# A gated recurrence followed by a binary feed-forward layer: one visit for four input chunks, another order in three iterations, paired blocks at the end, one more idle product

## The chip, the core and the metric

The kernel runs on one core of a Trainium2 chip. A core has TensorE (PE: matrix products into PSUM; its weight loads are shown as PEld), VectorE (DVE), ScalarE (ACT), GpSimd (POOL) and SyncE (SP). Each works through its own queue in order, and they wait for each other by semaphores. Transfers between the main memory and the on-chip memory SBUF are issued by SyncE and ScalarE and carried by 16 DMA engines. The metric is the device time of one execution in microseconds (us), lower being better; the figure to be predicted is the median over the runs.

## What is computed

The input x has 2 sequences of 4096 tokens of 256 numbers. The first layer is a gated recurrence with 64 states, the second a feed-forward layer with binary weights; each has a residual and a layer norm.

```python
u = x @ W_in + b_in                       # 256 -> 64
g = sigmoid(x @ W_gate + b_gate)          # 256 -> 256
h_t = tanh(h_{t-1} @ A + u_t @ Bm)        # along each sequence
y_t = g_t * (h_t @ C.T + u_t @ D.T) + (1 - g_t) * x_t
x1 = layernorm(2 * x + y @ W_out + b_out)
h = gelu(x1 @ (alpha1 * sign(w1)).T + b1) # 256 -> 1024
out = layernorm(x1 + h @ (alpha2 * sign(w2)).T + b2)
```

## The kernel before

**Tiling.** Each sequence is cut into 64 segments of 64 tokens, and all segments of both sequences advance together. One step of the recurrence is then one product for 128 columns (`steps`, line 156) and one tanh on ScalarE (line 158), and step after step depends on the one before. 48 warm-up steps over the last three quarters of each segment give the start states (`first_states`, line 161, copies them), and 64 steps follow: 112 in all. If a comparison at the end (`compare`, lines 166 to 172) finds that the warm-up was too short, a slow branch redoes everything; it is not taken here. The work beside the recurrence is cut into 16 chunks of 512 columns, each four positions of all segments.

**A chunk's work** is a list of pieces: u (line 131, read out of PSUM by VectorE in line 144), gates (line 313, tanh in line 361), `mix` (the y product, line 370, and the subtraction d, line 377), `mix_end`, `project` (W_out in two halves, line 395; then x1 and its statistics, line 406 and class `Stats`), `shift` and `norm` (layer norm; ScalarE, line 279), `turn` (transposes, line 423; ScalarE copies the high part xhi, line 431, VectorE subtracts to get the low part xlo, line 433), `rest` (adds b2 on GpSimd), four times `up` (products with sign(w1), line 451; gelu, line 458; high part hhi, line 467), `low` (low part hlo on VectorE, line 474) and `down` (products with sign(w2), line 490; after the last, VectorE scales out of PSUM into o, line 506), and at last `add` (line 512), `stats` and `store` (line 281 or 279, output in line 527). High and low parts keep single precision with a faster product format. The input of mix goes through a tile hu, which two transfers fill from the states (upper half) and from u (lower half), lines 342 to 349.

**PSUM.** The pool p_1 has three buffers, which u, gates and up share. p_m has one: mix, project and turn take turns in it, and each waits until the one before has been read. p_2 has one, for down.

**Order.** TensorE, ScalarE, VectorE and GpSimd run in the order in which the code emits (line 629); SyncE's queue is ordered by the compiler. `emit` (line 601) puts steps between pieces: each piece adds its cost (a table: a u visit 2000, a part of the gates 640, others 860) to a counter, and when it passes a pace one step is emitted, if u of its chunk is there. In the early stage the pace is 500, so that each part of a gate and each visit of u is followed by one step; later it is 5600. When 4, 8 and 12 of the 64 steps are out, the hu transfers of chunks 0, 1 and 2 are issued.

**Stages.** At the start six idle products (line 154) run while the first input and W_in load. Then seven rounds follow (lines 636 to 655): one part of the gates, a visit of u for a pair of chunks, x loads, and parts of the gates; on VectorE the weights are made into signs (`prepare_w`). The order of the pairs is (5, 6), (7, 8), (9, 10), (11, 12), (13, 14), (15, 0), (1, 2). After the first mixes and projections the main loop runs with c from 0 to 14: up, low, down of chunks c and c-1, mix of c+2, turn of c+1, project of c+2. In iterations 1 to 12 the gates of a later chunk stand behind the addition and statistics of chunk c-1. The last chunk, 15, ends in `down_end`, which works on one block of 128 rows at a time: products, scale, addition (GpSimd for the first three blocks, VectorE for the last), statistics of the block before, store of the one before that.

Of the kernel before, what the change touches and what calls it, by code (L numbers as in the profile page):

```python
# [19 lines left out]
KH = H // P  # L20
# [7 lines left out]
TB = N // P  # L28
# [4 lines left out]
EARLY = 500  # L33
# [4 lines left out]
def gated_recurrence_then_binary_ffn(  # L38
# [16 lines left out]
    nc = tc.nc  # L55
# [68 lines left out]
    def u_of_chunks(*chunks):  # L124

        n = N * len(chunks) // 2
        parts = [(chunks[0], 0), (chunks[1], 0) if len(chunks) == 2 else (chunks[0], 1)]
        ps = p_1.tile([P, N], FP, tag="h", name=f"ps_u{chunks[0]}")
        for k in range(KD):
            for (c, i), r in zip(parts, (LOW, TOP)):  # L130
                nc.tensor.matmul(  # L131
                    ps[r, :n],
                    w_in[k],
                    x_tiles[c][:, k, bass.ts(i, n)],
                    start=k == 0,
                    stop=k == KD - 1,
                    skip_group_check=True,
                )
        for (c, i), r in zip(parts, (LOW, TOP)):
            to = u_of[:, bass.ds(c * SPC + i * n // W, n // W)].rearrange("p j b k -> p (j b k)")  # L140
            if r is TOP and c == FIRST:
                nc.scalar.activation(to, ps[r, :n], AF.Identity, bias=bin_c[r, :])
            else:
                nc.vector.tensor_scalar(to, ps[r, :n], bin_c[r, :], None, ALU.add)
        have_u.update(chunks)
        yield
# [4 lines left out]
    def idle_products(n):  # L151

        for _ in range(n):
            nc.tensor.matmul(p_h, ones, ones, start=True, stop=True)
# [174 lines left out]
    class Chunk:  # L329
# [180 lines left out]
        def add(self, blocks=range(TB), engine=nc.vector):  # L510
            cut = slice(blocks[0], blocks[-1] + 1)
            engine.tensor_tensor(
                self.x1[:, cut, :], self.x1[:, cut, :], self.o[:, cut, :], ALU.add
            )
            yield
# [27 lines left out]

        def down_end(self):

            self.st2 = Stats(self.x1, f"b{self.nm}")
            for tb in range(TB + 2):
                one, before = range(tb, tb + 1), range(tb - 1, tb)
                if tb < TB:
                    for j in range(KH // 2, KH):  # L550
                        self.down_part(j, tb)
                    self.scale(one)
                    yield from self.add(one, nc.gpsimd if tb < TB - 1 else nc.vector)
                if 1 <= tb <= TB:
                    for what in (self.st2.gather, self.st2.merge, self.st2.root):
                        what(before)
                if tb >= 2:
                    engine = nc.scalar if tb < TB else nc.vector
                    queue = nc.scalar if tb % 2 else nc.sync
                    yield from self.store(range(tb - 2, tb - 1), engine, queue)  # L560

        def redo(self):

# [37 lines left out]
    def emit(what, pieces, pace=5600):  # L601
        nonlocal since
        for _ in pieces:
            since += COST.get(what, 0)
            if since >= pace:
                since = min(since - pace, pace // 2)
                if ready():
                    next_steps()

    def do(i, what, *args, pace=5600):  # L610
        if not 0 <= i < len(ch):
            return
        if what == "load":
            need = WARM + (ch[i].c + 1) * SPC
            while done < need:
                next_steps()
            ch[i].load()
        elif what in ("load_x", "load_gate_x"):
            getattr(ch[i], what)()
        else:  # L620
            emit(what, getattr(ch[i], what)(*args), pace)
# [7 lines left out]
    with tc.manual_schedule(engines={ET.PE, ET.Activation, ET.DVE, ET.Pool}):  # L629
        waiting = []  # L630
        for c in range(FIRST + 1, FIRST + 6):
            load_xT(c)
        idle_products(6)
        emit("u", u_of_chunks(FIRST), 1 << 30)
        since = 0
        pairs = [(5, 6), (7, 8), (9, 10), (11, 12), (13, 14), (15, 0), (1, 2)]
        loads = [[10, 11], [12, 13], [14, 15, 0], [1, 2], [3], [], []]
        for n, pair in enumerate(pairs):
            before = 2 if n == 0 else 1
            parts(before, EARLY)  # L640
            emit("u", u_of_chunks(*pair), EARLY)
            for c in loads[n]:
                load_xT(c)
            if n == 0:
                load_weights()
            if n == 3:
                halve_weights()
            if n >= 5:
                load_xT(n + 3)
            for i in range(7 - before):  # L650
                if 1 <= n < 5 and i == 0:
                    load_w(n - 1)
                if 2 <= n < 6 and i == 3:
                    prepare_w(n - 2)
                parts(1 if (n, i) != (6, 5) else 0, EARLY)
        assert done >= WARM + SPC, done
        emit("u", u_of_chunks(3), EARLY)
        for i in range(4):
            ch[i].xt = x_tiles[i]
        do(0, "mix", pace=850)  # L660
        do(0, "mix_end")
        parts(1, 600)
        assert done >= WARM + 2 * SPC, done
        do(1, "mix", pace=850)
        do(1, "mix_end")
        parts(1, 600)
        do(0, "project", 0, p_2, "o", pace=1700)
        do(0, "project", 1, pace=1700)
        assert done >= WARM + 3 * SPC, done
        do(2, "mix", pace=1700)  # L670
        do(0, "shift")
        do(1, "project", 0, p_2, "o", pace=1700)
        do(0, "norm")
        do(1, "project", 1, pace=1700)
        mixed = ch[2].mix_end()
        next(mixed)
        parts(2, 1700)
        while waiting:
            next_steps()
        waiting = None  # L680
        do(0, "turn", True)
        emit("", mean_w2())
        do(1, "norm", nc.vector)
        do(0, "rest")
        next(mixed)
        parts(2, 1700)
        for i in (4, 5):
            do(i, "load_x")
        end = len(ch) - 1
        parts_met = compare()  # L690
        late = gates(ch[10:], TB)
        for c in range(end):
            do(c + 6, "load_x")
            if c % 2 == 0:
                do(10 + c // 2, "load_gate_x")
            do(c, "up", 0)
            do(c, "low", 0)
            do(c - 1, "down", 2)
            do(c + 3, "load")
            if c > 0:  # L700
                do(c + 1, "shift")
                do(c + 1, "norm")
                do(c + 2, "mix")
                do(c + 2, "mix_end")
            do(c, "up", 1)
            do(c - 1, "down", 3)
            do(c - 1, "add", range(TB), nc.gpsimd if c == end - 1 else nc.vector)
            if c < end - 1:
                do(c - 1, "stats")
            if 1 <= c <= 12:  # L710
                emit("gate", (next(late, None) for _ in range(KD)))
            do(c + 1, "turn")
            do(c, "low", 1)
            do(c + 1, "rest")
            do(c, "up", 2)
            do(c, "low", 2)
            if c == end - 1:
                do(c - 1, "stats")
            else:
                do(c - 1, "store")  # L720
            if c == end - 2:
                assert done == len(plan), done
                next(parts_met)
                next(parts_met)
            do(c, "down", 0)
            do(c + 2, "project", 0)
            do(c, "up", 3)
            do(c, "down", 1)
            do(c, "low", 3)
            if c == end - 1:  # L730
                do(c - 1, "store")
            do(c + 2, "project", 1)
            if c == end - 2:
                next(parts_met)
                next(parts_met)
        count()
        do(end, "up", 0)
        do(end, "low", 0)
        do(end - 1, "down", 2)
        do(end - 1, "down", 3)  # L740
        do(end, "up", 1)
        do(end - 1, "add")
        do(end - 1, "stats")
        do(end, "low", 1)
        do(end, "up", 2)
        do(end, "low", 2)
        do(end, "down", 0, True)
        do(end, "up", 3, True)
        do(end - 1, "store", range(TB), nc.scalar)
        do(end, "low", 3, True)  # L750
        do(end, "down", 1)
        do(end, "down_end")
# [64 lines left out]
```

## Time and profile before

| | before |
|---|---|
| median of 3 runs | 452.75 us (452.65 to 454.31) |
| the profiled execution | 453.36 us, span 451.5 us |
| mean granted TensorE clock | 0.995 |
| TensorE busy | 439.7 us, 97% of the span |
| VectorE busy | 358.0 us, 79% |
| ScalarE busy | 261.1 us, 58% |
| GpSimd busy | 176.2 us, 39% |
| memory traffic | 44.51 MB, mean 99 GB/s |

The profile is of one execution. Its span runs from the first to the last event that it holds; the device time is 1.86 us longer. In a timeline line the first number is the start in us from the span's start, the second the duration in us (for several instructions joined in one line, until the end of the last); then come the engine (with q for a queue that issues transfers), the line of the kernel, the operation, the tile written and those read, shapes, and how many instructions the line joins. In brackets stands the idle time before it and what ended that. A product in plain single precision leaves two records for each call.

### The profile page before, as it was taken

What the parts mean: (1) busy time and instruction counts of PE and PEld (TensorE: products, weight loads), DVE (VectorE), ACT (ScalarE), POOL (GpSimd) and SP (SyncE); (2) the same over time, 40 slices, a digit from 0 to 9 for tenths busy, and PEclk for the clock granted to TensorE, in tenths of its full rate; (3) what the DMA queues carried; (4) which work ended last, traced back from release to release, by engine and by line L of the source; (5) the groups of instructions that cost most, each with busy time, mean ns of one, the idle gap of its engine ahead of it and who ended that gap; (6) DMA issues with size and microseconds to landing.
All of it is one profiled execution on the core that took longest, in us unless ns stands there. A gap on an engine that the chain in (4) does not pass through costs nothing.

```text
span 451.5 us, 6729 instructions
## 1 busy us (share of the span) xinstructions
PE 439.7 (97%) x2504; PEld 357.6 (79%) x2504; DVE 358.0 (79%) x600; ACT 261.1 (58%) x424; POOL 176.2 (39%) x179
## 2 busy tenths in 40 slices
PE   8999999999999999999999999999999999989992
PEld 5665666788888888887978787979788888879982
DVE  0245737976989798989898988899898989896775
ACT  2343442485657575757574747566666656556772
POOL 1001300553545434343445454535353545451713
PEclk9999999999999999999999999999999999999997
DMA  8898814321133322322232312212112020201012
GB/s 302 267 330 305 292 36 137 102 83 23 48 105 106 107 59 94 116 94 70 93 103 70 105 52 89 76 52 67 47 37 81 13 93 1 93 1 48 1 46 100
DMA packets 14838, 44.51 MB, mean 99 GB/s; under 512 B 2000, under 2 KB 3024, under 8 KB 14800
## 3 DMA queue, kind: packets, MB, share of 16 engines
q1 hardware_dynamic: 14224, 43.65, 29.1%
q8 instruction: 22, 0.36, 0.3%
q10 hardware_dynamic: 576, 0.37, 0.3%
q14 instruction: 16, 0.13, 0.1%
HBM read 31.43 MB, written 8.39 MB: 88 GB/s over the span
## 4 chain that ended last, share of the span: by engine, by line
PE 92%; DVE 5%; DMA 1%; ACT 1%; issue 0%; POOLq 0%; POOL 0%
PE ps_h L451 25%; PE ps_o L490 24%; PE ps_z L395 12%; PE ps_g L313 12%; PE ps_y L370 6%; PE ps_s L157 6%; PE ps_u L131 4%; PE ps_t L423 3%; DMA wab<-in_W_in_AB 1%; DVE bs_b L256 1%; DVE hlo L474 1%; DVE d L382 1%; DVE d L377 1%; DVE xlo L433 1%; DVE o L506 0%; PE ps_p L490 0%
## 5 line engine op out<-in xcount | busy, mean ns | idle before, releaser
L458 ACT ACTIVATE h<-ps_h,bias_c,al 128x512 f32<-128x512 f32 x128 | 97.5, 775 | 80.4 <-PE ps_h L451 75.2
L490 PE MATMUL ps_o<-sg,hhi 128*128 128x256 f32 x496 | 120.3, 282 | 0.0
L490 PE MATMUL ps_o<-sg,hlo 128*128 128x256 f32 x496 | 119.0, 279 | 0.1
L474 DVE TENSOR_TENSOR hlo<-h,hhi 128x1024 fp32r<-128x1024 f32 (+1 forms) x65 | 84.5, 1318 | 23.6 <-ACT hhi L467 23.5
L490 PEld LDWEIGHTS ps_o<-sg,hhi 128*128 128x128 f32 x496 | 93.6, 189 | 2.3
L490 PEld LDWEIGHTS ps_o<-sg,hlo 128*128 128x128 f32 x496 | 93.4, 188 | 2.5 <-DVE hlo L474 0.3
L451 PE MATMUL ps_h<-xhi,sg 128*128 128x512 f32 x256 | 92.2, 441 | 0.0
L451 PE MATMUL ps_h<-xlo,sg 128*128 128x512 f32 x256 | 80.2, 394 | 0.2
L355 POOL TENSOR_TENSOR xn<-xn,bo_r 128x256 f32<-128x256 f32 x64 | 59.3, 957 | 48.4 <-DMA xn<-in_x 48.4
L355 POOL TENSOR_TENSOR xn<-xn,b_r 128x256 f32<-128x256 f32 x64 | 75.5, 1208 | 1.2 <-PE ps_t L423 1.2
L467 ACT CAST hhi<-h 128x1024 fp32r<-128x1024 f32 (+1 forms) x65 | 67.3, 1037 | 2.0
L313 PE MATMUL ps_g<-xt,w_gate 128*128 128x384 f32 (+3 forms) x208 | 67.9, 438 | 0.0
L266 POOL TENSOR_TENSOR rs_a<-rs_a,neg_half 128x4 f32<-128x4 f32 x16 | 17.2, 1076 | 122.2 <-DVE rs_a L265 103.4
L395 PE MATMUL ps_z<-w_out,tg 128*128 128x256 f32 x256 | 61.1, 380 | 1.5 <-DVE xlo L433 1.5
L158 ACT ACTIVATE st<-ps_s 64x128 f32<-64x128 f32 x112 | 30.0, 267 | 56.0 <-PE ps_s L157 55.6
L451 PEld LDWEIGHTS ps_h<-xlo,sg 128*128 128x128 f32 x256 | 48.1, 188 | 11.9 <-DVE xlo L433 0.9
L157 PEld LDWEIGHTS ps_s<-st,wab 128*128 128x128 f32 x224 | 38.0, 192 | 24.0 <-issue 9.9
L451 PEld LDWEIGHTS ps_h<-xhi,sg 128*128 128x128 f32 x256 | 46.1, 189 | 12.7 <-issue 6.2
L266 POOL TENSOR_TENSOR rs_b<-rs_b,neg_half 128x4 f32<-128x4 f32 (+1 forms) x19 | 19.3, 1017 | 89.2 <-DVE rs_b L265 77.0
L395 PEld LDWEIGHTS ps_z<-w_out,tg 128*128 128x128 f32 x256 | 46.0, 190 | 6.8 <-DVE xlo L433 1.7
L279 ACT ACTIVATE xn<-xn,nm_a,rs_a 128x256 f32<-128x256 f32 x60 | 31.2, 591 | 24.5 <-DVE nm_a L271 24.5
L157 PE MATMUL ps_s<-st,wab 128*128 128x128 f32 x224 | 44.6, 281 | 0.1
(73 smaller groups left out, 482.9 us busy)
## 6 DMA issues: line engine op xcount, KB each, us to landing
xt<-in_xT SPq DMA_DIRECT2D x35, 512.0 KB, 4.3
xn<-in_x SPq DMA_DIRECT2D x16, 512.0 KB, 3.4
out_y<-xn SPq DMA_DIRECT2D x15, 512.0 KB, 2.6
hu<-st SPq DMA_DIRECT2D x32, 128.0 KB, 2.3
w1t<-in_w1T SPq DMA_DIRECT2D x2, 512.0 KB, 5.9
w1n<-in_w SPq DMA_DIRECT2D x2, 512.0 KB, 6.1
w2t<-in_w2T SPq DMA_DIRECT2D x2, 512.0 KB, 4.9
xt<-in_xT SPq DMA_DIRECT2D x2, 256.0 KB, 3.5
```

The source lines that it names most:

```text
L157: nc.tensor.matmul(p_h, ab, st[:, j].rearrange("p b k -> p (b k)"), start=True, stop=True)
L158: nc.scalar.activation(h_of[:, j + 1].rearrange("p b k -> p (b k)"), p_h[TOP, :], AF.Tanh)
L266: nc.gpsimd.tensor_tensor(rs, rs, neg_half[:, cut], ALU.pow)
L279: nc.scalar.activation(r, r, AF.Identity, bias=self.sh[:, i : i + 1], scale=rs)
L313: nc.tensor.matmul(ps[:, cut], w_gate[:, k, bass.ts(m, P)], xt_[:, k, cut], start=k == 0 and i == 0, stop=k == KD - 1, skip_group_check=True,)
L355: nc.gpsimd.tensor_tensor(r[:, i, :], r[:, i, :], row, ALU.add)
L395: nc.tensor.matmul(self.ps_z[:, i, :], self.y[:, k, bass.ts(i, P)], w_out[:, k, :], start=k == 0, stop=k == KD - 1,)
L451: nc.tensor.matmul(ps, sg1[:, k, bass.ts(j, P)], part[:, k, :], start=n == 0, stop=n == 2 * KD - 1,)
L458: nc.scalar.activation(h[:, i, :], ps, AF.Gelu, bias=b1_c[:, j : j + 1], scale=al1[:, j : j + 1],)
L467: nc.scalar.copy(hi[:, part, :], h[:, part, :])
L474: nc.vector.tensor_sub(lo[:, i, :], h[:, i, :], hi[:, i, :].bitcast(FP))
L490: nc.tensor.matmul(ps[:, i, :], part[:, j % 2, bass.ts(tb, P)], sg2[:, j, :], start=j == 0 and part is self.h[j // 2][0] and first, stop=j ...
```

## The change

Four edits. (1) Seven idle products are issued at the start instead of six. (2) The visit of u that takes chunks 13 and 14 also takes 15 and 0; it is followed by one step. The sixth round has no visit, and so no step behind one. (3) In main-loop iterations without gates (0, 13 and 14) the addition and the statistics of chunk c-1 are emitted behind `turn` of c+1 and the first `low` after it, instead of ahead of them. (4) `down_end` is written anew: blocks 0 and 1, and blocks 2 and 3, share aggregation calls, one reciprocal root for both and one shift; the statistics of a block are taken behind the scaling of the next one where there is one.

```diff
         def down_end(self):
 
-            self.st2 = Stats(self.x1, f"b{self.nm}")
-            for tb in range(TB + 2):
-                one, before = range(tb, tb + 1), range(tb - 1, tb)
-                if tb < TB:
-                    for j in range(KH // 2, KH):
-                        self.down_part(j, tb)
-                    self.scale(one)
-                    yield from self.add(one, nc.gpsimd if tb < TB - 1 else nc.vector)
-                if 1 <= tb <= TB:
-                    for what in (self.st2.gather, self.st2.merge, self.st2.root):
-                        what(before)
-                if tb >= 2:
-                    engine = nc.scalar if tb < TB else nc.vector
-                    queue = nc.scalar if tb % 2 else nc.sync
-                    yield from self.store(range(tb - 2, tb - 1), engine, queue)
+            st2 = self.st2 = Stats(self.x1, f"b{self.nm}")
+
+            def products(tb):
+                for j in range(KH // 2, KH):
+                    self.down_part(j, tb)
+                self.scale(range(tb, tb + 1))
+
+            def add(tb):
+                for _ in self.add(range(tb, tb + 1), nc.gpsimd if tb < TB - 1 else nc.vector):
+                    pass
+
+            def store(tb, engine):
+                cut = slice(tb, tb + 1)
+                st2.apply([tb], engine)
+                queue = nc.scalar if tb % 2 else nc.sync
+                queue.dma_start(out=self.at(out, self.c)[:, cut, :], in_=self.x1[:, cut, :])
+
+            for tb in range(2):
+                products(tb)
+                add(tb)
+            st2.gather([0])
+            products(2)
+            add(2)
+            st2.gather([1])
+            st2.merge([0, 1])
+            st2.root([0, 1])
+            products(3)
+            add(3)
+            st2.shift([0, 1])
+            store(0, nc.scalar)
+            store(1, nc.scalar)
+            st2.gather([2, 3])
+            st2.merge([2, 3])
+            st2.root([2, 3])
+            store(2, nc.vector)
+            store(3, nc.vector)
+            yield
...
-        idle_products(6)
+        idle_products(7)
...
-        pairs = [(5, 6), (7, 8), (9, 10), (11, 12), (13, 14), (15, 0), (1, 2)]
+        pairs = [(5, 6), (7, 8), (9, 10), (11, 12), (13, 14), (), (1, 2)]
...
-            emit("u", u_of_chunks(*pair), EARLY)
+            if pair:
+                emit("", u_of_chunks(*pair))
+                if pair == (13, 14):
+                    emit("", u_of_chunks(15, 0))
+                emit("u", [None], EARLY)
...
-            do(c - 1, "add", range(TB), nc.gpsimd if c == end - 1 else nc.vector)
-            if c < end - 1:
-                do(c - 1, "stats")
+            def add():
+                do(c - 1, "add", range(TB), nc.gpsimd if c == end - 1 else nc.vector)
+                if c < end - 1:
+                    do(c - 1, "stats")
+
             if 1 <= c <= 12:
+                add()
                 emit("gate", (next(late, None) for _ in range(KD)))
             do(c + 1, "turn")
             do(c, "low", 1)
+            if not 1 <= c <= 12:
+                add()
             do(c + 1, "rest")
```

## The prediction

> **What bounds the kernel.** I read the page first: busy shares, then the chain of work that ended last.
>
> ```profile
> PE 439.7 (97%) x2504; PEld 357.6 (79%) x2504; DVE 358.0 (79%) x600; ACT 261.1 (58%) x424; POOL 176.2 (39%) x179
> ...
> PE 92%; DVE 5%; DMA 1%; ACT 1%; issue 0%; POOLq 0%; POOL 0%
> ```
>
> TensorE is the busiest engine and 92% of the chain. The change takes no product out, so it can gain only where TensorE stands still, runs slowly, or has ended already. The timeline has four such places, one for each part. The start, on TensorE:
>
> ```profile
> 1.00 2.93 PE L154 MATMUL ps_s<-ones 128*128 128x128 f32 x12 [1.00 <-POOL ones L107]
> 4.32 1.97 PE L131 MATMUL ps_u<-xt,wab 128*64 128x256 f32 x8 [0.39 <-DMA wab<-in_W_in_AB]
> 9.93 1.97 PE L131 MATMUL ps_u<-xt,wab 128*64 128x512 f32 x8
> ```
>
> 256 columns take as long at 4.32 us as 512 columns at 9.93: up to about 10 us the array runs at half rate. The second place is the early stage, where a visit of u is slotted between recurrence steps (TensorE, ScalarE, SyncE's queue, VectorE):
>
> ```profile
> 51.16 1.94 PE L131 MATMUL ps_u<-xt,wab 128*64 128x512 f32 x8
> ...
> 59.10 0.30 ACT L161 COPY st<-st 64x126 f32<-64x126 f32 x1
> ...
> 68.41 5.75 SPq L349 DMA_DIRECT2D hu<-st  x4
> ...
> 70.06 1.23 DVE L377 TENSOR_TENSOR d<-ps_y,xt 128x1024 f32<-128x1024 f32 x1 [1.37 <-PE ps_y L370]
> ```
>
> The third is iteration 13, VectorE's timeline with TensorE's wait under it:
>
> ```profile
> 395.49 1.21 DVE L506 TENSOR_TENSOR o<-ps_o,al_r 128x1024 f32<-128x1024 f32 x1
> 396.73 1.23 DVE L512 TENSOR_TENSOR xn<-xn,o 128x1024 f32<-128x1024 f32 x1
> 398.00 1.41 DVE L256 BATCH_NORM_STATS2 bs_b<-xn 128x6 f32<-128x256 f32 x4
> ...
> 399.79 1.22 DVE L433 TENSOR_TENSOR xlo<-ps_t,xhi 128x1024 fp32r<-128x1024 f32 x1
> 400.92 2.88 DVE L474 TENSOR_TENSOR hlo<-h,hhi 128x1024 fp32r<-128x1024 f32 x2
> ...
> 408.55 1.22 DVE L406 SCALAR_TENSOR_TENSOR xn<-xn,ps_z 128x1024 f32<-128x1024 f32 x1 [0.50 <-PE ps_z L395]
> ...
> 401.06 1.99 PE L395 MATMUL ps_z<-w_out,tg 128*128 128x256 f32 x8 [1.53 <-DVE xlo L433]
> ```
>
> The projection waits for xlo to leave the one p_m buffer; xlo stands behind addition and statistics. This is the largest hole in the loop: 1.70 us beyond pitch. The fourth is the end, VectorE alone after the last product at 443.25:
>
> ```profile
> 444.44 0.42 DVE L512 TENSOR_TENSOR xn<-xn,o 128x256 f32<-128x256 f32 x1
> ...
> 446.33 0.40 DVE L281 TENSOR_SCALAR xn<-xn,mv_b,rs_b 128x256 f32<-128x256 f32 x1
> 447.17 0.41 DVE L281 TENSOR_SCALAR xn<-xn,mv_b,rs_b 128x256 f32<-128x256 f32 x1 [0.44 <-POOL rs_b L266]
> ```
>
> **The seventh idle product.** At half rate one costs two records of 0.213 us. The sixth streams until 3.72 and W_in lands so that u starts at 4.32; the seventh runs 3.72 to 4.14, inside that wait: cost 0 (0.05 if a draining product held up the weight load). What it may buy is the clock. The trace's clock record has entries at 10.09 (full) and 446.99 (half), 436.90 us apart, which is 128 times 3.413 us, and the matmul pitches turn at the same 10.1. So the clock is decided on a grid, here 3.26, 6.68, 10.09. From the records' starts, the window 6.68 to 10.09, after which it rose, held 0.30 us without streaming (91% busy). The window before held 0.60 (3.72 to 4.32) and 0.14 (6.08 to 6.22): 78%, and no rise. With the seventh, 0.60 becomes 0.17, so 91% as well, and the rise comes at 6.68. [...] By the row, work from 6.68 halves: u of (5, 6) would be due at 8.4, but xt6, issued at 2.6, took 6.5 us and lands at 9.1. So u runs 9.15 to 10.86 and the next step starts at 10.96, not 11.84: **-0.88**. [...]
>
> **One visit for four chunks.** TensorE's u work stays. Around a visit the pitches exceed the columns by 0.10 before, 0.05 at the first pair, 0.10 after and 0.11 in the first step, 0.36; a second u in the same visit adds about 0.02. So **-0.34**. At the sixth pair there is no visit and no step. Counting the pacing with 2000 for the visit and 640 per part, every later step moves back by one slot; the last takes a free slot in iteration 11, behind 351 us, at the same 0.21 us, and none is forced. The copy of line 161 then falls under u of (1, 2): before, step 48 waited for it, 0.29 and 0.08 beyond pitch; now 1.7 us of products cover it: **-0.36**. The h halves of hu0, hu1 and hu2 also issue one slot later on SP's queue. hu0: its step's tanh ends at 65.21 on the old clock, 2.2 us to land, 67.4, and mix of chunk 0 starts at 67.8: covered. hu1: 69.49 + 2.2 = 71.7, mix of chunk 1 started at 71.34, when d had freed p_m at 71.29: a new wait of **+0.39**, with all of TensorE behind it. VectorE isn't hurt: its next subtraction started at 73.97 behind its own work. hu2 has 3 us to spare. In p_1 the two u take two of three buffers and the open gate product the third; the next gate product at about 47.0 takes that of chunks 13, 14, which VectorE has read at 46.3: 0. Were it that of 15, 0 (read at 48.0), it would be +1.05. VectorE's 1.54 us in front of the weight preparation hide, as those signs are first multiplied after 90 us. Sum **-0.31**.
>
> **Low part ahead of addition.** Iterations 1 to 12 keep their order, iteration 0 has nothing to add, and in 14 the addition is on GpSimd, whose order is unchanged. In 13, xlo starts when xhi is copied, 396.93, and ends at 398.15, before the projection is due at 399.36: 1.70 us gone. But VectorE has no gap from 395.49 to 408.05, and the work is the same. Redone in the new order at the old pitches (xlo 1.13, low 1.14, addition 1.26, statistics 1.79, low 1.2, four applications 2.58, the two comparison steps 0.52, low 1.35 beside GpSimd's additions, which now run 403.4 to 408.3), line 406 starts at about 407.95 instead of 408.55, although its products end at 406.6. From there its statistics, low part and shift take 4.74 us (4.89 before, with a wait for hhi that is gone) and ScalarE's norm 2.3, so turn of chunk 15 starts at 415.02 instead of 415.87. TensorE, due at 414.0, stands 1.0 us there; the gelu of chunk 14's second step is queued behind norm on ScalarE, as before, and comes with it. The store of chunk 12 leaves SP's queue at 406.1 instead of 406.4, with nothing near behind it. So half the stall is passed on: **-0.85** (ends: -0.3 if GpSimd slows VectorE more, -1.7 if VectorE kept up). Behind turn, TensorE runs without a hole to 423.8, and all shifts.
>
> **Pairs at the end.** With the end's own pitches: statistics of block 1 end at 443.22, both aggregates 443.44, root input 443.63, third addition 444.41, the power of two columns at 0.71 (between 0.56 for one and 1.02 for four) until 444.41, shift 444.6, statistics of 2 and 3 until 445.27, root input 445.68, power 446.47, applications until 446.91 and 447.25. The last store issues at 447.29 on ScalarE's queue instead of 447.62; that of block 2 at 446.94 instead of 446.76 on SP's. Before they took 2.8 and 3.3 us to land, so the last landing is 450.24 instead of 450.42, or 450.1 by the first. Gain 0.18 to 0.33: **-0.28**. First stores come later by up to 0.6 but have landed before.
>
> **Sum.** -0.88 - 0.31 - 0.85 - 0.28 = -2.32. The profiled execution took 453.36 (span 451.5 and 1.86 around): 451.04. The median shown is 452.75, 0.61 less, which the grid's phase can give (a lucky phase already has part of the 0.88) or not: 450.43. I predict **450.8**, -0.43%. About 0.5% is what a measurement can tell here from no change: below 450.49 is faster.
>
> **Rivals.**
> - The seventh product does nothing, the rise stays at 10.1. [...] Against: 91% sufficed in the window that this trace shows. Without the 0.88: 451.7. Chance 0.17.
> - VectorE keeps up in iteration 13, or hu1 lands in time, with another 0.4 to 0.85: 450.0. For: it is idle 0.5 us before 408.55. Against: its unbroken row. Chance 0.18.
> - A buffer wait takes the gain: +1.05 at the double visit, or line 406 no earlier: 451.8 to 452.3. Chance 0.09.
> - Slower: with the faster start TensorE idles 0.75 us for xt6 inside 6.68 to 10.09, and the clock falls again at 10.09. Each window at half rate costs 1.7 us: one leaves 452.8, from the second on it is slower than before, and three give 456. Against: the hole at 399 lay within one window too, and the matmuls after it run at full pitch. Chance 0.04.
>
> The likeliest, all four parts at about these sizes, has 0.52 and its own range of 450.1 to 451.5, of which some 0.2 lies below 450.49. With 0.17 of the second rival and a little of the first, faster is 0.39; slower 0.04; same 0.57. The range drops half of the extremes: 449.6 to 452.4.
>
> **What would show it.** u of (5, 6) near 9.1 and steps at 0.11 pitch from 6.7; one u group of 16 records near 42, mix of chunk 1 waiting for the hu load by about 0.4; no wait of ps_z on xlo at 399 but one of turn on the norm near 413; VectorE's last application about 0.3 us nearer to the last product. Wrong if the rise stays at 10.1, if VectorE starts line 406 right behind its products, or if a gate product waits after the double visit.

## The result and the profile after

| | before | after |
|---|---|---|
| median of 19 runs each | 453.35 us | 452.41 us |
| ratio, 95% interval | 1 | 0.9985 (0.9973 to 0.9997) |
| the profiled execution | 453.36 us, span 451.5 | 452.42 us, span 450.6 |
| TensorE busy | 439.7 us | 439.4 us |

The change gains 0.15%, 0.68 us with an interval of 0.14 to 1.22 (the medians lie 0.94 apart; the ratio counts in one run of 455.7 us, of which more below). The forecast was 450.8, a gain of 2.32 us counted against the profiled execution; between the two profiled spans the gain is 0.83. The sign was right, and the change stayed within 0.5%, but most of the forecast gain is missing.

The page of the changed kernel, its first and fourth part:

```profile
PE 439.4 (98%) x2506; PEld 357.2 (79%) x2506; DVE 358.7 (80%) x597; ACT 261.2 (58%) x424; POOL 173.6 (39%) x177
...
PE 88%; DVE 6%; ACT 2%; DMA 2%; POOL 1%; issue 0%; POOLq 0%; DVEq 0%
```

TensorE does the same work. Its share of the chain fell from 92% to 88%, and those of VectorE, ScalarE, GpSimd and the DMAs rose by a point each: the chain leaves TensorE in more places than it did. To see where, I took the start of the same product (the n-th product into the same PSUM tile) in both traces and subtracted. A minus is a lead of the changed kernel:

| place (time before) | lead | step of the prediction |
|---|---|---|
| u of (5, 6), 9.9 | -1.33 | clock |
| u of (7, 8), 17.5 | -0.93 | clock: -0.88 forecast |
| u of (11, 12), 34.4 | -0.54 | 0.39 given back at 33 |
| first mix, 67.9 | -1.47 | visit: -0.93 so far |
| mix of chunk 1, 71.3, and on up to 343 | -1.00 | +0.49 for a load of hu |
| mix of chunk 15, 389.4 | -0.73 | +0.24, a step taken later: visit -0.20 net, -0.31 forecast |
| projection of chunk 15, 401.1 | -2.42 | iteration 13: -1.69 so far |
| last chunk's first up, 424.1 | -0.75 | all of it given back: -0.85 forecast |
| last product, 443.0 | -0.75 | |
| end of the span | -0.83 | end: -0.08, -0.28 forecast |

The start and the double visit on TensorE's timeline:

```profile
1.00 3.35 PE L154 MATMUL ps_s<-ones 128*128 128x128 f32 x14 [1.00 <-POOL ones L107]
4.34 1.97 PE L131 MATMUL ps_u<-xt,wab 128*64 128x256 f32 x8
...
7.63 0.82 PE L313 MATMUL ps_g<-xt,w_gate 128*128 128x128 f32 x4
...
8.61 2.37 PE L131 MATMUL ps_u<-xt,wab 128*64 128x512 f32 x8
...
33.01 0.67 PE L313 MATMUL ps_g<-xt,w_gate 128*128 128x256 f32 x2 [0.23 <-DMA xt<-in_xT]
...
42.23 3.65 PE L131 MATMUL ps_u<-xt,wab 128*64 128x512 f32 x16
...
70.37 1.10 PE L370 MATMUL ps_y<-hu,cd 128*128 128x512 f32 x2 [0.72 <-DMA hu<-st]
```

The seven products fill the wait for W_in; u at 4.34 no longer waits. From 7.63 on products run at full rate (the four records at 7.63 take 0.82 us, the same four at 8.09 before took 1.49), against 10.1 before. The first u of (5, 6) takes 2.37 us where 1.97 was usual: it stands 0.40 us in its middle, so the loaded input is the bound, as forecast. At 33.01 a gate product waits for chunk 0's input. The 16 records at 42.23 are the double visit, and no gate product waits behind it. At 70.37 mix of chunk 1 waits for its states.

Iteration 13 on VectorE's timeline, and under it GpSimd's:

```profile
396.21 1.23 DVE L433 TENSOR_TENSOR xlo<-ps_t,xhi 128x1024 fp32r<-128x1024 f32 x1 [0.19 <-ACT xhi L431]
...
398.48 1.22 DVE L512 TENSOR_TENSOR xn<-xn,o 128x1024 f32<-128x1024 f32 x1
...
401.54 1.22 DVE L474 TENSOR_TENSOR hlo<-h,hhi 128x1024 fp32r<-128x1024 f32 x1
403.67 3.06 DVE L281 TENSOR_SCALAR xn<-xn,mv_b,rs_b 128x256 f32<-128x256 f32 x4 [0.91 <-POOL rs_b L266]
...
408.30 1.21 DVE L406 SCALAR_TENSOR_TENSOR xn<-xn,ps_z 128x1024 f32<-128x1024 f32 x1
```

```profile
401.77 1.86 POOL L266 TENSOR_TENSOR rs_b<-rs_b,neg_half 128x4 f32<-128x4 f32 x1 [7.97 <-DVE rs_b L265]
403.61 2.96 POOL L355 TENSOR_TENSOR xn<-xn,b_r 128x256 f32<-128x256 f32 x4
```

xlo now comes ahead of the addition. But the applications of chunk 12's store (line 281), which need the power of line 266, wait 0.91 us, since the power took 1.86 us; before, it took 1.02. Line 406 starts at 408.30, although TensorE had written its operand by about 406.0:

```profile
404.10 1.89 PE L395 MATMUL ps_z<-w_out,tg 128*128 128x256 f32 x8
```

What the late line 406 does to TensorE is in the view of waits between 384 and 424 us (who waits for whom, the time, how often, the longest), before and after:

```profile
PEld ps_z L395 <- DVE xlo L433: 1.7, 1, 1.7
PE ps_z L395 <- DVE xlo L433: 1.5, 1, 1.5
```

```profile
PEld ps_t L423 <- ACT xn L279: 1.7, 4, 0.6
PE ps_t L423 <- ACT xn L279: 0.9, 4, 0.4
```

The wait of the projection for xlo is gone, and one of the transposes of chunk 15 for ScalarE's norm, block by block, has come: 1.69 us left the projection and 1.7 arrived at the turn.

The end, all engines:

```profile
443.04 0.71 POOL L266 TENSOR_TENSOR rs_b<-rs_b,neg_half 128x2 f32<-128x2 f32 x1
...
445.10 1.86 ACTq L561 DMA_DIRECT2D out_y<-xn  x2
...
445.84 0.73 DVE L281 TENSOR_SCALAR xn<-xn,mv_b,rs_b 128x256 f32<-128x256 f32 x2 [0.81 <-POOL rs_b L266]
```

The power of two columns took the 0.71 us that had been interpolated. The last store's issue starts 4.38 us after the start of the last product, against 4.65: 0.27 of the forecast 0.33. But the store landed 3.0 us later instead of 2.8.

### The profile page after: what moved, and what is told of

It is laid out like the page before. It is cut to its first block, busy times and chain, and to the rows that moved or that the text cites. A ratio compares the mean times of both kernels' runs of the same rounds, so it can differ in the third digit from the quotient of the medians.

```text
span 450.6 us, 6727 instructions
## 1 busy us (share of the span) xinstructions
PE 439.4 (98%) x2506; PEld 357.2 (79%) x2506; DVE 358.7 (80%) x597; ACT 261.2 (58%) x424; POOL 173.6 (39%) x177
## 4 chain that ended last, share of the span: by engine, by line
PE 88%; DVE 6%; ACT 2%; DMA 2%; POOL 1%; issue 0%; POOLq 0%; DVEq 0%
PE ps_h L451 24%; PE ps_o L490 23%; PE ps_z L395 12%; PE ps_g L313 11%; PE ps_y L370 6%; PE ps_s L157 5%; PE ps_u L131 4%; PE ps_t L423 3%; DVE hlo L474 1%; DMA xt<-in_xT 1%; ACT xn L279 1%; DVE xn L281 1%; PE ps_s L154 1%; ACT h L458 1%; DVE bs_a L256 1%; ACT hhi L467 1%
## 5 line engine op out<-in xcount | busy, mean ns | idle before, releaser
L355 POOL TENSOR_TENSOR xn<-xn,bo_r 128x256 f32<-128x256 f32 x64 | 60.7, 979 | 45.5 <-DMA xn<-in_x 45.5
L355 POOL TENSOR_TENSOR xn<-xn,b_r 128x256 f32<-128x256 f32 x64 | 71.5, 1145 | 1.2 <-PE ps_t L423 1.2
```

Of the source, the lines that this page charges most:

```text
L355: nc.gpsimd.tensor_tensor(r[:, i, :], r[:, i, :], row, ALU.add)
```

## The experiments

The theory after the result: the clock's share was a property of one execution, iteration 13's share is lost because VectorE's queue order holds line 406, and the visit is as forecast apart from a wait for hu. The rivals: the idle product truly gives 0.9 us and what comes later takes it back (the wait for chunk 0's input as its price); line 406 is held by something other than the store ahead of it; the wait for hu is chance. The experiments came in three groups, each on a chip of its own beside new runs of the kernel before (medians 452.96, 453.03 and 453.03). Leads are counted against the one profile before.

**Each edit alone.** Only the idle product:

```diff
-        idle_products(6)
+        idle_products(7)
```

> The kernel before with seven idle products and nothing else changed. Theory (the clock window): the clock record's rise comes about 3 us earlier than the 10.05 us of the kernel before (somewhere in 4.4 to 7.8, as the grid falls), u of chunks 5 and 6 starts near 8.6 to 9.2 and ends near 10.9 instead of 11.8, so TensorE is 0.9 us ahead at 12 us. But the gate products of chunk 0 then wait for its x load near 32.6 us by about 0.4, as in the changed kernel, so only 0.5 us reaches the end: ratio 0.9989. Rival (the earlier rise was the grid's chance phase in that one execution): rise again near 10, nothing gained, ratio 1.000. Second rival (the x0 wait comes from the moved visit of u, not from the faster start): no wait at 32.6 us, 0.9 us gained at the end, ratio 0.998.

14 runs: median 452.31 against 452.96, ratio 0.9988 (0.9976 to 1.0000). The clock's record rises at 4.9, u of (5, 6) starts at 8.18, and the lead over the profile before is 1.17 us at 42 us. The interval takes in the 0.9989 expected and reaches the rival's 1.000. The gate product near 33 hardly waits for chunk 0's input (0.05 us instead of the 0.4 expected), though it comes earlier than in the changed kernel. There that load took 5.5 us from issue to landing, in the other executions 4.6 to 5.4, and where it took over 5.2 (the later mix and no idle products, below) 0.1 and 0.3 us were lost as well: the wait at 33 goes with the time of that transfer and is not the price of the start.

Only the visit:

```diff
-        pairs = [(5, 6), (7, 8), (9, 10), (11, 12), (13, 14), (15, 0), (1, 2)]
+        pairs = [(5, 6), (7, 8), (9, 10), (11, 12), (13, 14), (), (1, 2)]
...
-            emit("u", u_of_chunks(*pair), EARLY)
+            if pair:
+                emit("", u_of_chunks(*pair))
+                if pair == (13, 14):
+                    emit("", u_of_chunks(15, 0))
+                emit("u", [None], EARLY)
```

> The kernel before with only the one visit of u for chunks 13, 14, 15 and 0. Theory: TensorE comes to the first mix 0.92 us earlier (0.34 for the second visit's overhead, 0.37 for the copy of the start states now under u of chunks 1 and 2, 0.21 for the step not yet taken), the mix of chunk 1 then waits 0.5 us more than before for the upper half of its hu, and the missing step costs 0.23 later, so 0.2 us are gained at the end of the products. Rival (a p_1 buffer is missing after the double visit): the gate product behind it waits about 1 us near 47 us. The clock rises near 10 us as before, and no x load is waited for at 32 to 34 us.

One execution, 452.29 us. Its lead grows from 0.98 to 1.91 by the first mix, shrinks to 1.44 when mix of chunk 1 waits 0.72 us for hu, and to 1.18 with the later step: 0.20 net, the same as in the full change. What was not expected is the start of this kernel, which has six idle products. TensorE's timeline:

```profile
1.00 2.93 PE L154 MATMUL ps_s<-ones 128*128 128x128 f32 x12 [1.00 <-POOL ones L107]
4.31 1.83 PE L131 MATMUL ps_u<-xt,wab 128*64 128x256 f32 x8 [0.38 <-DMA wab<-in_W_in_AB]
...
7.51 0.82 PE L313 MATMUL ps_g<-xt,w_gate 128*128 128x128 f32 x4
8.17 0.38 PE L157 MATMUL ps_s<-st,wab 128*128 128x128 f32 x2
8.48 2.09 PE L131 MATMUL ps_u<-xt,wab 128*64 128x512 f32 x7
```

The wait for W_in is there, and yet the array runs at full rate from before 7.5 on; the clock's record has the rise at 5.9. Six products don't mean a rise near 10.

Only the order:

```diff
+            def add():
+                do(c - 1, "add", range(TB), nc.gpsimd if c == end - 1 else nc.vector)
+                if c < end - 1:
+                    do(c - 1, "stats")
+
             if 1 <= c <= 12:
+                add()
...
             do(c, "low", 1)
+            if not 1 <= c <= 12:
+                add()
```

> The kernel before with only the addition and statistics moved behind the low part in iteration 13. Theory (the hole is handed on, because the x1 of chunk 15, line 406, stands in VectorE's queue behind the applications of chunk 12's store, which wait for a power that GpSimd takes 1.9 us for beside VectorE's low part): the 1.7 us wait of the projection for xlo at 401 us is gone, line 406 starts 1.5 us or more after its products end, and turn of chunk 15 waits for the norm until TensorE's lead is 0.1 us or less: ratio 1.000. Prediction on record: lead of 0.85 us at turn, ratio 0.998.

14 runs: 452.87 against 452.96, ratio 1.0003 (0.9992 to 1.0014). The lead is 0.83 ahead of iteration 13, 2.53 at the projection, and 0.79 at the last chunk's first up. The gain is made and lost inside this one edit; the others have no part in it. The power again takes 1.86 us, from 401.65.

Only the new `down_end` (the part of the diff above that concerns it):

> The kernel before with only the new end of the last chunk. Theory: the last store is issued about 0.27 us sooner after the last product than before (4.37 us), but takes 0.2 us longer to land, as the store before it is issued only 0.33 us earlier; the span is shorter by less than 0.15 us. Prediction on record: 0.28 us.

One execution, 452.13 us. The last issue comes 4.37 us after the last product's start, 0.28 earlier than before; the landing took 3.2 us and the span ends 8.59 behind that product, against 8.50. The issue moved as forecast and the landing took it back in this execution.

**What holds line 406.** The changed kernel, with chunk 12's store moved behind the norm of chunk 15 in the queues:

```diff
                 do(c + 1, "norm")
+                if c == end - 1:
+                    do(c - 2, "store")
...
-            else:
+            elif c != end - 2:
                 do(c - 1, "store")
```

(c is the loop's chunk, end is 15; the first two new lines act at c = 14, the last keeps the store out of c = 13)

> The changed kernel with one more move: in iteration 13 the store of chunk 12 (four applications on VectorE and one transfer) is emitted behind the norm of chunk 15 in iteration 14. Theory (line 406 is late because VectorE's queue holds the applications and their wait for GpSimd's power in front of it): line 406 starts right behind its products, near 406 us, turn of chunk 15 no longer waits, and TensorE keeps the whole 1.7 us: lead at the end of the products 1.6 us over the changed kernel, ratio to the kernel before 0.995. Rival (GpSimd's additions slow VectorE, or the norm on ScalarE is what turn waits for): line 406 still starts more than 1 us behind its products or turn still waits over 1 us; ratio 0.9985 as for the changed kernel.

6 runs: 450.65 against 453.03, ratio 0.9951 (0.9934 to 0.9969). VectorE's timeline:

```profile
405.40 1.22 DVE L406 SCALAR_TENSOR_TENSOR xn<-xn,ps_z 128x1024 f32<-128x1024 f32 x1
...
410.23 0.15 DVE L271 SCALAR_TENSOR_TENSOR nm_a<-mv_a,rs_a 128x4 f32<-128x4 f32 x1
410.31 1.38 DVE L281 TENSOR_SCALAR xn<-xn,mv_b,rs_b 128x256 f32<-128x256 f32 x4
412.70 1.22 DVE L506 TENSOR_TENSOR o<-ps_o,al_r 128x1024 f32<-128x1024 f32 x1 [1.02 <-PE ps_o L490]
```

Line 406 starts 2.9 us earlier, 0.69 of which this execution was ahead anyway. The applications cost nothing behind the norm: they take 1.38 us instead of 3.06, and VectorE still waits 1.02 us for TensorE after them. In the profiles before and after, such four applications take 1.38 at the two places where no GpSimd instruction runs beside them (427.01 and 426.04), and 2.63 to 3.06 at the 28 where GpSimd's additions do. No transpose of chunk 15 waits for the norm any more, and the last chunk keeps 1.77 us more lead than in the changed kernel. So it was the store in VectorE's queue that held line 406.

The same move in the kernel before, without the new order:

> The kernel before with only the store of chunk 12 moved behind the norm of chunk 15. Theory (two cuts are needed, since xlo and line 406 are held by different pieces of the same queue): the projection still waits 1.7 us for xlo at 401 us, line 406 starts behind its products as before, and nothing is gained after 395 us (0.1 us at most). Rival (the store was the only burden): turn comes up to 1.7 us earlier.

One execution, 453.38 us. Two lines of its timeline, TensorE's and VectorE's:

```profile
400.29 1.99 PE L395 MATMUL ps_z<-w_out,tg 128*128 128x256 f32 x8 [1.58 <-DVE xlo L433]
```

```profile
407.84 1.22 DVE L406 SCALAR_TENSOR_TENSOR xn<-xn,ps_z 128x1024 f32<-128x1024 f32 x1 [0.55 <-PE ps_z L395]
```

The projection still waits for xlo, and line 406 then waits for the projection. The lead over the profile before stays (0.84 ahead of the iteration, 0.77 at the projection and at the last product): the move alone gives nothing. The two edits are worth 1.8 us together and nothing each. By the way, mix of chunk 1 waited 0.62 us for hu here, although the visit is as before: its transfers landed up to 3.2 us after issue. In ten of the twelve profiled executions it was 2.2 to 2.4.

The changed kernel, with chunk 13's second low part too ahead of the addition, to have no low part beside the power:

```diff
+            if c == end - 2:
+                add()
+                do(c + 1, "rest")
```

(behind the second `low`; for this iteration the calls at the old places are left out)

> The changed kernel with, in iteration 13, the low part of the third step also ahead of the addition, so that GpSimd's power of chunk 12 no longer starts beside a VectorE operation that reads two SBUF operands. Theory (such a start makes the power take 1.9 us instead of 1.0): the power takes 1.02 us, but nothing lies between it and the applications now, so these wait about 1.1 us and line 406 starts within 0.3 us of where the changed kernel has it; no gain at turn. Rival (the power is slow there for another reason): 1.86 us again, and line 406 a microsecond later still.

One execution, 455.48 us. VectorE's timeline in iteration 13, then GpSimd's:

```profile
406.74 3.04 DVE L281 TENSOR_SCALAR xn<-xn,mv_b,rs_b 128x256 f32<-128x256 f32 x4 [1.20 <-POOL rs_b L266]
...
411.36 1.20 DVE L406 SCALAR_TENSOR_TENSOR xn<-xn,ps_z 128x1024 f32<-128x1024 f32 x1
```

```profile
405.69 1.02 POOL L266 TENSOR_TENSOR rs_b<-rs_b,neg_half 128x4 f32<-128x4 f32 x1 [9.54 <-DVE rs_b L265]
```

The power is back at 1.02, so the low part beside it was what had made it 1.86. But now VectorE has nothing to do meanwhile and waits 1.20. Counted from the same lead, line 406 comes 0.72 us later than in the changed kernel, where within 0.3 had been expected, and the turn 0.71. Shortening the power doesn't pay by this order.

The other 2.35 us by which this execution is longer are 3.27 lost near 71 us, where its code is that of the changed kernel, less 0.92 by which it was ahead at 42. Its timeline on TensorE, and then the view of stretches (from:to, us, busy time of each engine, granted clock, DMA share, GB/s):

```profile
71.04 1.15 PE L370 MATMUL ps_y<-hu,cd 128*128 128x512 f32 x2 [2.32 <-DMA hu<-st]
```

```profile
68.50:72.00 3.50, 1.18 (x5) 0.53 (x5) 2.84 (x3) 0.27 (x1) 0.00 (x0) 0.99 0.26 59
72.00:75.40 3.40, 3.40 (x11) 2.29 (x10) 1.03 (x1) 0.54 (x2) 0.00 (x0) 0.51 0.45 154
75.40:80.00 4.60, 4.60 (x25) 4.08 (x24) 2.88 (x4) 0.61 (x3) 0.00 (x0) 1.00 0.42 93
```

The two transfers of hu landed 3.8 and 3.5 us after issue instead of 2.2, so TensorE stood for 2.32 of the 3.41 us up to 72.0. There the clock's record falls to half, and it rises again at 75.4. The wait cost 1.61 us more than in the changed kernel, the stretch at half rate 1.66. The late transfer was paid twice.

**The wait for hu.** The changed kernel, with one more part of the gates ahead of mix of chunk 1 and none behind it:

```diff
-        parts(1, 600)
+        parts(2, 600)
...
-        parts(1, 600)
```

> The changed kernel with the second gate part (and its step) ahead of the mix of chunk 1 instead of behind it. Theory (the mix waits for the transfer of the upper half of hu, which issues one slot later): the wait of 0.9 us in front of the mix of chunk 1 falls to 0.1 or less, and TensorE comes to the first projection 0.5 to 0.9 us sooner against the visit of u of chunks 1 and 2. Rival (the mix waits for d to free p_m): the wait stays above 0.4.

One execution, 452.15 us. TensorE's timeline:

```profile
69.29 0.82 PE L313 MATMUL ps_g<-xt,w_gate 128*128 128x128 f32 x4
69.95 0.38 PE L157 MATMUL ps_s<-st,wab 128*128 128x128 f32 x2
70.26 1.10 PE L370 MATMUL ps_y<-hu,cd 128*128 128x512 f32 x2
```

No wait is left. Against the changed kernel the lead grows by 0.80 from the first mix to the first projection: the wait's own 0.49, and the rest from the part of the gates that no longer stands behind it. At the last product 0.65 of it is left. The wait is there in all three executions that have the visit and the mix where the change puts them and transfers of the usual 2.2 us (the changed kernel, the visit alone, the late store), and the later mix avoids it.

**All together.** The changed kernel, with the late store and the later mix, and chunk 0's input ahead of chunk 15's:

```diff
-        loads = [[10, 11], [12, 13], [14, 15, 0], [1, 2], [3], [], []]
+        loads = [[10, 11], [12, 13], [14, 0, 15], [1, 2], [3], [], []]
```

> The changed kernel with the late store, the second gate part ahead of the mix of chunk 1, and the x load of chunk 0 issued ahead of that of chunk 15. Theory: the gains add, 1.6 us from the store and 0.5 to 0.9 us from the mix, and no wait for the x load of chunk 0 near 32.6 us: ratio to the kernel before 0.9935 (450.0 us where that has 453.0). If either wait only moves on, 0.995 to 0.9985.

8 runs: 450.08 against 453.03, ratio 0.9947 (0.9928 to 0.9965): faster than the kernel before and, by its ratio, than the changed kernel, and the best version found. Its products end 2.86 us ahead of those of the changed kernel, 0.47 of which it was ahead at 42 us. That it beats the late store alone (0.9951) is not shown by these intervals.

**No idle products.** The kernel before, without them:

```diff
-        idle_products(6)
+        idle_products(0)
```

> The kernel before without any idle product. Theory (a grid window of 3.41 us whose array time is about 0.8 or more busy raises the clock; the grid lies at random from one execution to the next, so six products already do it in most executions): no window that begins before about 3.7 us can be busy enough now, so the rise lies between 7.1 and 10.6 us in every execution, and the median is 0.3 to 0.9 us longer: ratio 1.0015. Rival (idle products do not matter to the clock, any rise time may come): a rise before 7 us is possible and the ratio is 1.000.

The 0.8 of the theory is an estimate: it lies between two windows of the profile before, 78% busy without a rise behind it and 91% with one. 22 runs: 453.26 against 453.03, ratio 1.0007 (0.9999 to 1.0016), which takes in the 1.0015 expected and the rival's 1.000. The record rises at 8.1, in the range expected. TensorE's timeline:

```profile
4.35 1.97 PE L131 MATMUL ps_u<-xt,wab 128*64 128x256 f32 x8 [4.35 <-DMA wab<-in_W_in_AB]
...
9.07 1.94 PE L131 MATMUL ps_u<-xt,wab 128*64 128x512 f32 x8
```

Even with the rise at 8, u of (5, 6) starts at 9.07, 0.31 us behind the landing of its input, and the lead over the profile before is 0.62 us at 42 us.

**The start over all executions.** For each profiled execution, the rise of the clock and the lead over the profile before at u of (13, 14), 42 us, which lies ahead of all edits but the idle products and, in e8, the order of two loads:

| idle products | rise of the clock, us | lead at 42 us |
|---|---|---|
| 6 (before; e2, e3, e4, e6) | 10.1; 5.9, 5.1, 4.0, 5.4 | 0; 0.98, 0.85, 1.20, 1.19 |
| 7 (after; e1, e5, e7, e8, e10) | 7.1; 4.9, 7.0, 4.6, 5.0, 7.1 | 0.54; 1.17, 1.21, 0.73, 1.01, 1.46 |
| 0 (e9) | 8.1 | 0.62 |

(e1 is the idle product alone, e2 the visit, e3 the order, e4 the pairs, e5 the late store, e6 it in the kernel before, e7 the later mix, e8 all together, e9 no idle products, e10 the low part ahead.) With six products the mean is 0.84, with seven 1.02. The seventh is worth about 0.2 us by this (0.3 if the lead is taken at 32 us, ahead of the wait for chunk 0's input), within a scatter of 0.5, so that nothing is not ruled out; the profile before was the worst of five with six products. Taken modulo 3.41 us, the rises lie anywhere from 0.2 to 3.3: the phase differs from execution to execution.

**The end over all executions.** The end of the span, counted from the last product's start, was 8.50, 8.80, 8.53, 9.17, 9.28 and 9.14 with the old `down_end` (before, e1, e2, e3, e6, e9), mean 8.90, and 8.42, 8.59, 8.47, 8.89, 8.46 and 8.42 with the new (after, e4, e5, e7, e8, e10), mean 8.54. The profile before was the shortest of six. The pairs are worth about 0.36 us: 0.25 in the issue (4.34 to 4.38 behind the last product's start, against 4.56 to 4.65), which is outside the scatter, and the rest in landings, which ran from 2.8 to 3.6 us in both sets and could be chance.

## Why the prediction was wrong

Two steps failed. Of the 1.64 us between the forecast and the measured gain, they account for about 0.7 and 0.85.

**The seventh idle product, -0.88: the first failed step.** In the trace of before alone, which has one interval, the step of 3.413 us was an assumption of mine; the later runs show it. Rise and fall of the record are 436.91 us apart in the profile before and 440.32 in the one after, which differ by 3.413 us and are 128 and 129 times that, and the half-rate stretch of the kernel with the low part ahead (72.0 to 75.4) lasts one such step. What failed was to take the phase of one execution for a property of the kernel: the sum allowed that the median may have a luckier phase, and kept the term whole. Four of five executions with six products rise between 4.0 and 5.9, without a seventh. By the table the term is about -0.2; timed alone, the edit gave -0.54 us with an interval of -1.09 to 0.00, which rules out none of 0, -0.2 and -0.88. So the rises of the other executions show what failed; how much the product is worth on average stays open. The rival "the seventh product does nothing" came nearest here, though for another reason than it gave: the rise does not stay at 10.1 but is mostly early anyway.

**Its reference.** The sum was made against the profiled execution, 453.36, which is near the median of 453.35 and so looks typical. It was so by two chances that partly cancelled: a start 0.8 us late and an end 0.4 us short, against the means above. A gain at the start read from it is too large, and one at the end too small.

**One visit, -0.31: right in mechanism, measured -0.20.** The visit's overhead and the copy gave the forecast gains, and the wait for hu of chunk 1 came, 0.49 instead of 0.39. The step taken later cost 0.24, forecast at 0.21. No buffer wait came behind the double visit.

**Low part ahead of addition, -0.85: the second failed step, measured 0.0** (in the profile, and 1.0003 timed alone). The chain of the argument was right: the wait for xlo went, and the turn waits for the norm. What failed is the redone queue "at the old pitches". From xlo's start to line 406 I had 10.97 us; it took 12.09. The difference is the wait of 0.91 for the power, and applications of 2.98 instead of 2.58 (from the start of the first to that of the next operation); the last low part was 0.21 shorter. The low part, now issued right behind the root's input, runs under the power, and that makes the power 1.86. This case had been seen in the trace of before, on VectorE and GpSimd:

```profile
87.26 1.22 DVE L382 SCALAR_TENSOR_TENSOR d<-tg,d 128x1024 f32<-128x1024 f32 x1
...
424.87 1.22 DVE L474 TENSOR_TENSOR hlo<-h,hhi 128x1024 fp32r<-128x1024 f32 x1
427.01 1.38 DVE L281 TENSOR_SCALAR xn<-xn,mv_b,rs_b 128x256 f32<-128x256 f32 x4 [0.91 <-POOL rs_b L266]
```

```profile
87.43 1.93 POOL L266 TENSOR_TENSOR rs_a<-rs_a,neg_half 128x4 f32<-128x4 f32 x1 [2.01 <-DVE rs_a L265]
...
425.04 1.93 POOL L266 TENSOR_TENSOR rs_b<-rs_b,neg_half 128x4 f32<-128x4 f32 x1 [0.58 <-DVE rs_b L265]
```

The second place is the very sequence that the change makes in iteration 13: the low part directly behind the root's input, the long power, and the applications waiting 0.91 us for it.

I took the power from the row of before at 400.02, 1.02 us, where xlo, which reads one operand from PSUM, stood beside it. The rival "line 406 no earlier" with 451.8 to 452.3 (chance 0.09, shared with a buffer wait) is what happened in this part: on the clock of before, line 406 started at 409.03 instead of 408.55.

**Pairs, -0.28: right for the issue, which moved by 0.25.** In the two profiles the end moved by only -0.08, since the profile before had the shortest end of its kind; over the executions by -0.36, landings included.

**The slower rival** did not decide the result, but its mechanism exists: the kernel with the low part ahead shows a clock that falls for one window after a wait of 2.3 us, at the price of 1.66 us where 1.7 had been worked out. It came at the hu load and not at the start. One of the 19 runs of the changed kernel took 455.7 us. Its mean granted clock was 0.990, against 0.993 to 0.996 in the others, and one window of 3.41 us at half rate takes 0.004 from the mean of its span: it fits one such window. Where that arose is open, as the run was not profiled.

With the terms as measured over the executions, -0.2 - 0.2 + 0 - 0.36, the sum is -0.76, a gain inside the timed 0.14 to 1.22.

## What to carry to other kernels

A term that depends on when the clock rises, which was anywhere from 4.0 to 10.1 us in these executions, needs several executions of the kernel before: one trace gives one draw, and a typical total does not make each part typical. When work on a full queue is reordered, take each duration from a row with the same neighbours on the other engines, not from the nearest row of the same instruction; and ask which optional work (here a store) still stands in front of the late step, for removing one wait paid only together with moving that.

## What the runs showed of the hardware

- The power of 128 x 4 on GpSimd took 1.02 to 1.03 us in 55 of the 62 rows of the profiles before and after. In the other seven, those that start under a VectorE operation of 128 x 1024 that reads two tensors from SBUF, it took 1.85 to 1.93. In three of these it ended 0.87 to 0.88 us after that operation's end (88.48 and 89.36 before; 402.76 and 403.63, 425.12 and 426.00 after). The other direction does not show: a low part that starts while a power runs (132.53 before, the power from 132.07) takes its usual 1.23 us.
- A stretch of 3.41 us in which TensorE stood for 68% was followed by one of 3.4 us at half rate (the kernel with the low part ahead, granted clock 0.51 from 72.0 to 75.4); in the changed kernel and in the visit alone the same wait, 0.72 us long, was not (granted clock 1.00 from 72.0 to 75.4 in the one; the next y product, at 71.08, in its usual 1.02 us in the other, against 1.92 at 72.42 with the low part ahead).
- The transfers of hu for chunk 1, 128 KB each, landed 2.2 to 2.4 us after issue in ten executions, 3.2 in one and 3.8 in one.
